# Attention and Mamba on one core: the Mamba layer's timetable drawn anew, with another first pair and another choice of products for GpSimd

## The chip, the core and the metric

The kernel runs on one core of a Trainium2 chip. A core has five engines with instruction queues of their own: TensorE (PE in the profile, its weight loads PEld), VectorE (DVE), ScalarE (ACT), GpSimd (POOL) and SyncE (SP), which here only issues DMAs. Each engine takes its instructions strictly in order, and an instruction starts when the semaphores that it waits for have been reached. The metric is the time of one execution on the device in microseconds; lower is better.

## The reference

A batch of 128 images of 128 channels and 32 x 32 pixels goes through two layers, all in fp32. The first is an attention over the batch at each pixel, with a residual and a layer norm. The second is a Mamba block on each image's 1024 pixels, taken as a sequence:

```python
xh = einsum('oi,bihw->bohw', cv1_w, x) + cv1_b
l  = silu(batchnorm(depthwise_conv3x3(xh)))
t  = layernorm(xh as tokens)
xm, z = split(t @ in_proj_w.T)                     # 256 channels each
xm = silu(causal_conv1d(xm, 4 taps) + conv1d_b)
dt, Bm, Cm = split(xm @ x_proj_w.T)                # 8, 16, 16
dt = softplus(dt @ dt_proj_w.T + dt_proj_b)
h[s] = exp(dt * A) * h[s-1] + dt * Bm * xm         # 256 channels x 16 states
y  = (h * Cm).sum(states) + xm * D
g  = (y * silu(z)) @ out_proj_w.T
out = x + cv2_w @ concat(l, g) + cv2_b
```

The costly part is the recurrence: 256 x 16 sequences of 1024 steps in each of 128 images.

## The kernel before

The attention layer runs first and leaves its result in DRAM (`mid`). It takes about the first 2900 us, and nothing in it is touched here. The Mamba layer then works on the images one after another, overlapped in time.

Of an image the recurrence makes 32 **units** of 128 x 1024: half `h` of the channels (two), group `nb` of four states (four), and block `db` of 32 channels (four). Two blocks form a pair, A (blocks 0 and 1) or B (2 and 3), and `PAIRS` (L367) lists the 16 pairs of an image in their order, such as `A1`: block pair A, states 1. Unit `k` belongs to pair `k // 2`. A unit consists of these tasks (`unit`, L1197, inside `units`, L1190):

- **decay k** on ScalarE (L1241): exp(dt x A) from `dtr`, the copy of dt that a load has spread to 128 partitions.
- its **inputs** dt x B x xm: for 20 units GpSimd makes two at once (`b_poolk`, L1216, `dtxr` times `brep` into one of three `dbu` buffers); for the 12 units of the pairs in `TENSOR` (L372) TensorE makes them by eight transposes of a prepared tile `bx` (`b_tensork`, L1209). TensorE writes into one of two PSUM tiles `da`, which alternate by unit. The decay takes the other place, `da` or `dbu`.
- **scan k** on VectorE (L1254): the recurrence itself.
- **product k**, h times C (L1262): on GpSimd for the units in `ON_POOL` (then the scan has written SBUF), on VectorE for the others (then the scan has written `da`).
- **sums** (L1281): for each half and state group, TensorE adds four units' products into `y_ps`. The products wait in eight `hc` buffers, taken in turn, so scan `k` may need the sums of unit `k - 8`.

Around the units stand, for the image itself, the `gate` (L1321), the sigmoid of z (`z_mm`, L909, into two PSUM banks, and `silu_z`, L926), `silu_l` and the outputs (`o_first`, `o_second`, `o_copy`); and for the next images the layer norm (`norm_mm`, `squared`, `variance`, `rstd`, `normed`), the causal convolution (`xm_mm`, `xm_copy`), the 3x3 convolution (`taps`, `l_copy`), and dt, B and C: `d_mm` (L954), `d_copy` (L970), `a_mm` (L983), four `softplus` (L998), `b_mm` and `b_copy` (L1045), then `dt_store`, `dtx_mul` on GpSimd (L1025) and `dtx_store`. ScalarE loads an activation table before the sigmoids, one after `silu_l`, one before softplus and one after it (1.28 us each).

dt, dt x xm, B and C are stored to DRAM and loaded again, spread over partitions, by SyncE's queue: `load_dt` and `load_dtx` (L1071, 1 MB each; two halves `j`, one for the A pairs and one for B, for each `h`), `load_b` and `load_c` (L1104, L1111, half a megabyte each).

The order on every engine is written out by hand or by a planner outside the file: the dictionary `AT` gives each task a moment in its image's timetable, and image `i` begins at `i * PERIOD`.

```python
t.at = t.image * PERIOD + AT[t.name]                       # L337
...
for t in sorted(self.tasks, key=lambda t: (t.at, t.place)):  # L356
```

The numbers only sort. The program is emitted in that order, so each engine's queue is that order, and when a task runs is left to the semaphores on the chip.

Of the kernel before, what the change touches and what calls it, by code (L numbers as in the profile page):

```python
# [324 lines left out]
class Plan:  # L325
# [43 lines left out]
    for h, some in enumerate(['A1 A2 B2 B1 A3 A0 B3 B0', 'A0 A1 B0 B1 A2 A3 B2 B3'])  # L369
# [7 lines left out]
ON_POOL = [0, 1, 2, 3, 5, 8, 10, 11, 12, 13, 14, 15, 18, 19, 23, 25, 26, 27]  # L377

PERIOD = 96.19
AT = {  # L380
    "a_mm00": -44.86, "a_mm01": -43.94, "a_mm10": -40.89, "a_mm11": -40.09, "b_copy": -37.27,
    "b_mm": -38.14, "b_pool0": -11.59, "b_pool6": 2.5, "b_pool8": 14.73, "b_pool12": 21.64,
    "b_pool18": 45.47, "b_pool22": 50.01, "b_pool24": 56.93, "b_pool26": 68.6, "b_pool28": 73.15,
    "b_pool30": 77.69, "b_tensor2": 2.41, "b_tensor3": 0.28, "b_tensor4": 6.97, "b_tensor5": 4.86,
    "b_tensor10": 29.61, "b_tensor11": 27.54, "b_tensor14": 38.87, "b_tensor15": 35.79,
    "b_tensor16": 43.3, "b_tensor17": 40.35, "b_tensor20": 56.91, "b_tensor21": 53.12,
    "bc_store": -31.86, "d_copy": -45.59, "d_mm": -47.72, "decay0": -2.15, "decay1": -5.96,
    "decay2": -0.53, "decay3": -11.29, "decay4": 7.68, "decay5": 3.95, "decay6": 17.31,
    "decay7": 12.43, "decay8": 24.71, "decay9": 18.35, "decay10": 28.35, "decay11": 27.31,
    "decay12": 34.25, "decay13": 31.47, "decay14": 29.39, "decay15": 30.43, "decay16": 38.19,  # L390
    "decay17": 37.15, "decay18": 51.1, "decay19": 48.51, "decay20": 47.47, "decay21": 52.14,
    "decay22": 63.5, "decay23": 61.02, "decay24": 69.99, "decay25": 67.67, "decay26": 75.38,
    "decay27": 72.31, "decay28": 81.79, "decay29": 77.7, "decay30": 89.02, "decay31": 83.25,
    "dt_store0": -40.28, "dt_store1": -10.23, "dtx_mul0": -34.72, "dtx_mul1": -2.29,
    "dtx_store0": -32.21, "dtx_store1": 9.24, "gate0": 49.49, "gate1": 108.33, "l_copy0": -3.86,
    "l_copy1": -4.92, "load_b0": -27.4, "load_b1": 22.22, "load_b2": -1.78, "load_c0": -3.58,
    "load_c1": -12.03, "load_c2": -7.18, "load_c3": 7.44, "load_dt00": -19.55, "load_dt01": -5.38,
    "load_dt10": 29.62, "load_dt11": 36.91, "load_dtx00": -22.92, "load_dtx01": -13.83,
    "load_dtx10": 19.4, "load_dtx11": 38.71, "norm_mm0": -132.98, "norm_mm1": -98.77,
    "normed0": -125.31, "normed1": -89.36, "o_copy0": 131.83, "o_copy1": 117.14,  # L400
    "o_first0": 126.95, "o_first1": 111.81, "o_second0": 129.82, "o_second1": 114.47,
    "out_store0": 132.7, "out_store1": 118.02, "pad_mm0": -92.28, "pad_mm1": -90.19,
    "padded0": -91.2, "padded1": -89.11, "product0": 19.27, "product1": 0.13, "product2": 12.35,
    "product3": 7.05, "product4": 13.35, "product5": 9.98, "product6": 20.99, "product7": 16.98,
    "product8": 28.5, "product9": 24.88, "product10": 33.6, "product11": 31.23,
    "product12": 38.35, "product13": 35.98, "product14": 43.09, "product15": 40.72,
    "product16": 48.27, "product17": 47.06, "product18": 63.86, "product19": 54.56,
    "product20": 61.3, "product21": 57.68, "product22": 67.81, "product23": 66.23,
    "product24": 73.72, "product25": 82.24, "product26": 91.53, "product27": 89.16,
# [1079 lines left out]
```

## Time and profile before

| | |
|---|---|
| time, median of 3 runs | 15043.29 us |
| lowest, highest | 15040.22, 15054.52 us |
| profiled execution: time, span | 15073.08 us, 15071.3 us |
| VectorE busy | 13733.7 us, 91% |
| TensorE busy | 13455.7 us, 89% |
| GpSimd busy | 12317.6 us, 82% |
| ScalarE busy | 12058.3 us, 80% |

The page shows one execution; the median is of other executions. Shares are over the whole span, attention included: in its first fifth GpSimd is hardly used, in the rest it is busy 9 tenths and more in every slice. A row of groups gives line, engine, operation, written and read tiles, shapes and count, then busy time in us and the mean of one in ns, then the idle time of the engine just before such instructions with what ended it. A row of the timeline gives start, duration, engine, line and tiles, and in brackets an idle time before it. In the view of windows the columns are the window, its length, the busy time of PE, PEld, DVE, ACT and POOL with their instructions, the granted TensorE clock, the DMA share and GB/s.

### The profile page before, as it was taken

To read this page: it belongs to the slowest core of one execution; us is meant where nothing else is said; L and a number is where in the kernel's file an instruction comes from. 1 tells how busy PE (TensorE), PEld (TensorE's weight loads), DVE (VectorE), ACT (ScalarE), POOL (GpSimd) and SP (SyncE) were. 2 spreads that over 40 slices of the span, in tenths; PEclk is the share of its full clock that TensorE was granted. 3 is DMA by queue.
4 is the path that set the end of the run, shared out by engine and by line. 5 is a ranking of instruction groups with operands and counts; after the bars stand their busy time and mean duration, and the time that the engine had idled before them with its cause. 6 is when DMAs were issued, how large, how long until landed. Compare 5 with 4: busy or idle time off the path is not lost. (4 is left out here: it accounts for less than half of the span.)

```text
span 15071.3 us, 229111 instructions
## 1 busy us (share of the span) xinstructions
PE 13455.7 (89%) x87094; PEld 6624.5 (44%) x87094; DVE 13733.7 (91%) x8754; ACT 12058.3 (80%) x19718; POOL 12317.6 (82%) x4361
## 2 busy tenths in 40 slices
PE   9999999888888888888888888888888888888887
PEld 6666666433333333333333333333333333333333
DVE  6777777599999999999999999999999999999999
ACT  5666666688888888888888888888888888888887
POOL 1222222299999999999999999999999999999999
PEclk9999999899999999999999999999999999999999
DMA  3222222266676666666666666666666666666665
GB/s 57 50 57 46 46 46 46 67 169 169 169 169 169 168 169 169 168 168 169 169 168 168 168 168 169 168 169 168 169 167 169 168 168 169 169 169 169 167 168 146
DMA packets 1191603, 2180.96 MB, mean 145 GB/s; under 512 B 673233, under 2 KB 674273, under 8 KB 1190497
## 3 DMA queue, kind: packets, MB, share of 16 engines
q1 hardware_dynamic: 1190496, 2166.31, 59.6%
q8 instruction: 682, 11.17, 0.3%
q14 instruction: 425, 3.47, 0.1%
HBM read 1746.30 MB, written 419.43 MB: 144 GB/s over the span
## 5 line engine op out<-in xcount | busy, mean ns | idle before, releaser
L1216 POOL TENSOR_TENSOR dbu<-dtxr,brep 128x2048 f32<-128x2048 f32 x1280 | 5805.4, 4552 | 27.7 <-DMA dtr<-dtd 13.3
L1262 POOL TENSOR_TENSOR hc<-hc,crep 128x1024 f32<-128x1024 f32 x2304 | 5412.3, 2372 | 310.5 <-PE da L1209 211.1
L1241 ACT ACTIVATE da<-dtr,aneg 128x1024 f32<-128x1024 f32 x2560 | 2956.6, 1163 | 510.3 <-DVE hc L1262 489.3
L1254 DVE TENSOR_TENSOR_SCAN hc<-da,dbu 128x1024 f32<-128x1024 f32 x1408 | 3162.1, 2276 | 103.6 <-ACT da L1241 94.9
L1155 ACT ACTIVATE bx<-p_ps,bT 128x128 f32<-128x128 f32 (+1 forms) x8192 | 2798.0, 486 | 132.1 <-PE p_ps L1147 131.9
L1254 DVE TENSOR_TENSOR_SCAN da<-da,dbu 128x1024 f32<-128x1024 f32 x1152 | 2622.7, 2287 | 115.3 <-ACT da L1241 106.9
L1209 PE MATMUL da<-ident,bx 128*128 128x128 f32 x12288 | 1828.7, 295 | 501.1 <-DVE hc L1254 417.6
L1209 PEld LDWEIGHTS da<-ident,bx 128*128 128x128 f32 x12288 | 1489.7, 150 | 1634.3 <-DVE hc L1254 1068.5
L1262 DVE TENSOR_TENSOR hc<-da,crep 128x1024 f32<-128x1024 f32 x1792 | 2162.8, 1219 | 47.8 <-PE y_ps L1281 6.5
L769 PE MATMUL p_ps<-tn,wk 128*128 128x512 f32 x4096 | 1989.5, 608 | 240.4 <-DVE tn L733 147.2
L1241 ACT ACTIVATE dbu<-dtr,aneg 128x1024 f32<-128x1024 f32 x1536 | 1734.3, 1218 | 473.2 <-DMA dtr<-dtd 471.1
L1254 DVE TENSOR_TENSOR_SCAN hc<-dbu,da 128x1024 f32<-128x1024 f32 x896 | 2000.1, 2268 | 24.3 <-ACT dbu L1241 21.4
L1281 PE MATMUL y_ps<-hc,fold 128*32 128x512 f32 x16384 | 1974.3, 599 | 37.6 <-POOL hc L1262 25.8
L1254 DVE TENSOR_TENSOR_SCAN da<-dbu,da 128x1024 f32<-128x1024 f32 x640 | 1451.1, 2282 | 196.4 <-PE da L1209 132.6
L221 POOL COPY xg<-xt 128x512 f32<-128x512 f32 x256 | 270.4, 1057 | 1223.2 <-PE m_ps L217 1199.3
L830 PE MATMUL p_ps<-xpad,dwd 64*64 64x512 f32 x9216 | 1153.4, 593 | 112.8 <-ACT xm L801 105.3
L769 PEld LDWEIGHTS p_ps<-tn,wk 128*128 128x128 f32 x4096 | 710.6, 191 | 1141.6 <-issue 776.3
L243 POOL TENSOR_SCALAR yt<-z,nw,nb 128x512 f32<-128x512 f32 x256 | 320.2, 1251 | 1032.7 <-DVE z L242 1032.7
L1281 PEld LDWEIGHTS y_ps<-hc,fold 128*32 128x32 f32 x16384 | 477.0, 109 | 1182.9 <-issue 858.3
L830 PEld LDWEIGHTS p_ps<-xpad,dwd 64*64 64x64 f32 x9216 | 362.4, 133 | 802.4 <-issue 568.4
L1025 POOL TENSOR_TENSOR dtt<-dtt,xm 128x1024 f32<-128x1024 f32 x256 | 608.5, 2377 | 120.9 <-DMA dtd<-dtt 109.8
L203 DVE TENSOR_TENSOR oT<-m_ps,rden 128x512 f32<-128x512 f32 x256 | 177.0, 691 | 566.2 <-ACT rden L202 566.2
(131 smaller groups left out, 19281.3 us busy)
## 6 DMA issues: line engine op xcount, KB each, us to landing
dtxr<-dtxd SPq DMA_DIRECT2D x2048, 256.0 KB, 5.5
dtr<-dtd SPq DMA_DIRECT2D x2048, 256.0 KB, 5.4
crep<-bcd SPq DMA_DIRECT2D x2048, 128.0 KB, 6.2
brep<-bcd SPq DMA_DIRECT2D x1536, 128.0 KB, 5.0
x<-mid SPq DMA_DIRECT2D x256, 512.0 KB, 5.9
dtd<-dtt SPq DMA_DIRECT2D x256, 512.0 KB, 5.2
dtxd<-dtt SPq DMA_DIRECT2D x256, 512.0 KB, 4.4
xt<-in_x SPq DMA_DIRECT2D x64, 1024.0 KB, 12.2
```

Of the source, the lines that this page charges most:

```text
L221: nc.gpsimd.tensor_copy(xgs[p % 4].rearrange("c (l b) -> c l b", l=LG), pixels(xts, p))
L243: nc.gpsimd.tensor_scalar(pixels(yts, y), z.rearrange("c (l b) -> c l b", l=LG), nw, nb, ALU.mult, ALU.add,)
L769: nc.tensor.matmul(a.tile, lhsT=wk[:, k, h * P : (h + 1) * P], rhs=tn[:, c * CH + k : (c + 1) * CH + k], start=k == 0, stop=c > 0 and k == ...
L830: nc.tensor.matmul(pair[r] .tile[c * HP : (c + 1) * HP] .rearrange("p (r q) -> p r q", q=HH), lhsT=dwd[rs, k, :], rhs=xpad[rs, y0 : y0 + r ...
L1025: lambda: nc.gpsimd.tensor_mul(dtt[h], dtt[h], im["xm"][h]),
L1155: nc.scalar.activation(bx[:, tb, ks, n, :], src, AF.Copy, scale=bT[:, j : j + 1])
L1209: nc.tensor.transpose(ps[:, tb * P : (tb + 1) * P], bx[:, tb, TENSOR[h, nb] * NDB + db].rearrange("p n d -> p (n d)"), ident,)
L1216: nc.gpsimd.tensor_mul(dbu[u // 2 % NDBU], dtxr[db // 2], brep[nb - 1].unsqueeze(1).to_broadcast([P, 2, L]),)
L1241: lambda: nc.scalar.activation(a, dtr[db // 2][:, db % 2, :], AF.Exp, scale=aneg[:, h * NDB + db, nb : nb + 1],),
L1254: lambda: nc.vector.tensor_tensor_scan(dst, a, b, 0.0, ALU.mult, ALU.add),
L1262: lambda: engine.tensor_mul(hc[u % 8], dst, crep[nb]),
L1281: nc.tensor.matmul(y_ps[db * GD : (db + 1) * GD, chunk(c)], lhsT=fold, rhs=hc[(i * NG + k) % 8][:, chunk(c)], start=False, stop=last,)
```

## The change

The two constants and the whole timetable are replaced; no function changes. In the first half of an image `A2` now comes before `A1`. So units 0 and 1 are units whose inputs TensorE makes (`b_tensor0`, `b_tensor1`), and units 2 and 3 have a pair of GpSimd's (`b_pool2`). `ON_POOL` has 19 units instead of 18: 4, 16, 21, 24 and 30 come in, 5, 15, 23 and 26 go out. `AT` has the same tasks but for those names, at other moments, and so another order on each engine. The core of the diff, with the lines that the prediction speaks of:

```diff
@@ -366,7 +366,7 @@
-    for h, some in enumerate(['A1 A2 B2 B1 A3 A0 B3 B0', 'A0 A1 B0 B1 A2 A3 B2 B3'])
+    for h, some in enumerate(['A2 A1 B2 B1 A3 A0 B3 B0', 'A0 A1 B0 B1 A2 A3 B2 B3'])
@@ -374,64 +374,64 @@
-ON_POOL = [0, 1, 2, 3, 5, 8, 10, 11, 12, 13, 14, 15, 18, 19, 23, 25, 26, 27]
+ON_POOL = [0, 1, 2, 3, 4, 8, 10, 11, 12, 13, 14, 16, 18, 19, 21, 24, 25, 27, 30]
-PERIOD = 96.19
+PERIOD = 94.66
...
-    "b_tensor16": 43.3, "b_tensor17": 40.35, "b_tensor20": 56.91, "b_tensor21": 53.12,
+    "b_tensor15": 41.17, "b_tensor16": 42.34, "b_tensor17": 47.31, "b_tensor20": 54.77,
+    "b_tensor21": 59.11, "bc_store": -43.47, "d_copy": -44.15, "d_mm": -46.19, "decay0": -2.38,
...
-    "sums10": 64.75, "sums11": 69.91, "sums12": 90.68, "sums13": 94.53, "taps0": -14.18,
+    "softplus11": -36.36, "squared0": -127.55, "squared1": -89.95, "sums00": 50.41,
+    "sums01": 27.39, "sums02": 22.78, "sums03": 43.48, "sums10": 67.78, "sums11": 75.14,
...
-    "xm_mm111": -86.2, "xm_mm112": -85.14, "xm_mm113": -84.09, "z_mm00": 36.94, "z_mm01": 37.97,
-    "z_mm10": 41.5, "z_mm11": 42.4,
+    "xm_mm113": -79.34, "z_mm00": 39.18, "z_mm01": 40.22, "z_mm10": 45.41, "z_mm11": 46.37,
```

The order that follows from it, around the places that the prediction works out (tasks of the next image marked with ', of the image after it with "):

| engine | before | after |
|---|---|---|
| TensorE | `b_tensor14`, `b_tensor17`, `z_mm10`, `z_mm11`, `b_tensor16`, `sums03`, `sums00`, `d_mm'`, `a_mm00'`, `a_mm01'`, `b_tensor21`, `a_mm10'`, `a_mm11'`, `b_tensor20`, `b_mm'`, `norm_mm0"` | `b_tensor15`, `b_tensor16`, `sums03`, `z_mm10`, `z_mm11`, `b_tensor17`, `d_mm'`, `sums00`, `a_mm00'`, `a_mm01'`, `b_tensor20`, `a_mm10'`, `a_mm11'`, `b_mm'`, `b_tensor21`, `norm_mm0"` |
| ScalarE | `silu_z10`, `silu_z11`, `silu_l`, decays 20 and 19, `d_copy'`, decays 18 and 21, softplus' (four), `b_copy'`, `squared0"`, decay 23, `rstd0"`, decay 22 | `silu_z10`, `silu_z11`, `silu_l`, `d_copy'`, decays 18, 19 and 20, softplus' (four), `b_copy'`, decay 21, `squared0"`, decay 22, `rstd0"`, decay 23 |
| GpSimd | products 13, 12, 15, 14, pairs 18, 22, product 19, pair 24, `dtx_mul0'`, products 18, 23, pairs 26, 28, 30, product 25, pair 0', products 27, 26 | products 13, 14, pair 18, product 16, pairs 22, 24, `dtx_mul0'`, products 21, 18, 19, pairs 26, 28, 30, products 25, 24, 27, 30, pair 2' |
| SyncE | `load_dtx01'`, `load_c1'`, `dt_store1'`, `load_c2'`, `load_dt01'` | `load_dtx01'`, `load_b2'`, `dt_store1'`, `load_c1'`, `load_dt01'` |

On VectorE each image's scans now run in the order of their numbers; before, the odd one of a pair mostly came first.

## The prediction

> **What bounds the kernel now.** I read the page first (engine totals, slices), then the groups between 4000 and 14000 us with shapes kept apart, then the busy time within one image, and last one image instruction by instruction. From slice 9 on the page repeats itself: 128 images in one rhythm. The same scan starts in image 119 99 x 94.63 us after it starts in image 20, so an image costs **94.63 us**, and all below is per image.
>
> The groups (busy us, mean ns | idle time before them, and who ended it), and the busy time within one image:
>
> ```profile
> L1216 POOL TENSOR_TENSOR dbu<-dtxr,brep 128x2048 f32<-128x2048 f32 x1057 | 4794.2, 4552 | 11.2 <-DVE da L1254 10.3 <-DMA dtxr<-dtxd 0.3 <-POOL hc L1262 0.2
> L1262 POOL TENSOR_TENSOR hc<-hc,crep 128x1024 f32<-128x1024 f32 x1904 | 4472.7, 2372 | 256.0 <-PE da L1209 173.3 <-DVE hc L1254 76.8 <-DMA brep<-bcd 0.4
> ...
> L1262 DVE TENSOR_TENSOR hc<-da,crep 128x1024 f32<-128x1024 f32 x1480 | 1786.3, 1219 | 36.3 <-PE y_ps L1281 2.2
> ```
> ```profile
> core 0: us, PE busy (x) PEld busy (x) DVE busy (x) ACT busy (x) POOL busy (x), PEclk, DMA share, GB/s
> 9007.13:9101.76 94.63, 82.31 (x420) 36.92 (x420) 90.84 (x50) 79.17 (x133) 91.85 (x31) 0.96 0.70 169
> ```
>
> VectorE (90.8) and GpSimd (91.9) both fill the image to 4%. Neither is the bound alone: each loses about 3 us to short waits on the other, on ScalarE, on TensorE and on the loads of `dtr`. A change that moves work between the two is decided by the waits it leaves.
>
> **The change, part by part.**
>
> *Products.* Five move to GpSimd (4, 16, 21, 24, 30), four come back to VectorE (5, 15, 23, 26). Back to back, GpSimd takes 2.33 us for a product (seven in 16.35; less the last one's 2.37, over six) and 4.49 for an input pair (three in 13.50). Its floor becomes 10 x 4.49 + 21 x 2.33 (19 products, two `dtx_mul`) = **93.8 us**; it was 91.5. VectorE loses 1.14 us, start to start, and needs 89.8. So GpSimd has the least room, and the gain can't pass 0.83 us.
>
> *A rule against it.* The row: the product takes 2.37 us on GpSimd and 1.22 on VectorE. The Trainium skill (GPSIMD Engine Reference, section 4.1, Engine selection) puts elementwise work on VectorE because of such a ratio. Obeyed, no product moves, and the sum stays at 94.63.
>
> *The pair order.* Units 0 and 1 now take their inputs from TensorE, units 2 and 3 from GpSimd; there are still 12 such units and ten pairs. The pair that opened the image was ready 5 us before its scan, so its going saves nothing by itself.
>
> *The timetable.* No task is added on TensorE, ScalarE or the load queue; their order is new. I followed it along GpSimd's queue with the trace's starts and durations, and asked of each product and pair when its inputs come if GpSimd never pauses. Most come early: product 8 by 4 us, 10 to 14 by 1.4 to 1.9, pairs 26, 28 and 30 by 3 or more, `dtx_mul0` and `dtx_mul1` by about 2. Those moves cost nothing while that lead lasts, and each us beyond it counts once per image. Two places have no lead.
>
> *Place 1, product 13 to product 21.* TensorE's new order is `b_tensor16`, `sums03`, `z_mm10`, `z_mm11`, `b_tensor17`, `d_mm`. `sums03` waits for product 13, and the second half of the gate's matmuls, ahead of it until now, is queued behind. Behind these on ScalarE stand the gate's sigmoids, `silu_l`, `d_copy`, decays 18 to 20, the softplus, `b_copy` and decay 21; scan 21 waits for that, and product 21, new on GpSimd, for the scan. The prices (start, duration):
>
> ```profile
> 9050.99 1.25 ACT L874 ACTIVATE l<-l,bnt,bns 128x1024 f32<-128x1024 f32 x1
> 9052.26 1.28 ACT L877 ACT_TABLE_LOAD   x1
> ...
> 9055.70 0.59 ACT L970 COPY xp<-p_ps 128x512 f32<-128x512 f32 x1
> 9056.18 1.13 ACT L1241 ACTIVATE da<-dtr,aneg 128x1024 f32<-128x1024 f32 x1
> 9057.24 1.14 ACT L1241 ACTIVATE dbu<-dtr,aneg 128x1024 f32<-128x1024 f32 x1
> 9058.39 1.28 ACT L998 ACT_TABLE_LOAD   x1
> 9059.68 1.27 ACT L998 ACTIVATE dtt<-p_ps,dtb 128x512 f32<-128x512 f32 x2
> 9062.35 1.45 ACT L998 ACTIVATE dtt<-p_ps,dtb 128x512 f32<-128x512 f32 x2 [1.40 <-PE p_ps L983]
> 9063.82 1.28 ACT L877 ACT_TABLE_LOAD   x1
> 9065.86 0.27 ACT L1045 COPY bT<-p_ps 128x32 f32<-128x32 f32 x2 [0.76 <-PE p_ps L1040]
> ```
>
> From product 13's end: 0.05 to the start of `sums03`, 1.74 for it, 1.96 to the end of `z_mm11` (all start to start on TensorE), 0.08 to the sigmoid, 0.57, 1.27 for `silu_l`, 1.30 for the table: `d_copy` at 6.97. Then 0.48, 1.05 + 1.05 (decays 18, 19), 2.44 (decay 20 and a table): softplus at 11.99. To its fourth part 2.67 + 0.76, then 1.99 (0.71 and a table; the 0.76 wait for `b_mm` goes, as `b_tensor21` no longer stands ahead of it), 0.2 for `b_copy`, 1.18 for decay 21, 2.27 for scan 21, 0.13 to GpSimd: **21.18**. GpSimd would be there after 3 x 4.49 + 3 x 2.33 = 20.46 (pairs 18, 22, 24, products 14, 16, `dtx_mul0`), less 0.02. It waits **0.74**.
>
> In that sum 2.67 + 0.76 is a price at half clock:
>
> ```profile
> 9056.34 1.13 PE L983 MATMUL p_ps<-xp,dtwT 8*128 8x512 f32 x4 [0.69 <-ACT xp L970]
> 9058.63 1.09 PE L1209 MATMUL da<-ident,bx 128*128 128x128 f32 x8 [1.16 <-DVE hc L1254]
> 9060.43 2.65 PE L983 MATMUL p_ps<-xp,dtwT 8*128 8x512 f32 x4 [0.70 <-ACT dtt L998]
> ```
> ```profile
> 9056.00:9060.00 4.00, 2.22 (x12) 1.16 (x12) 4.00 (x3) 3.97 (x5) 4.00 (x2) 1.00 0.01 2
> 9060.00:9063.00 3.00, 2.57 (x4) 0.81 (x4) 2.97 (x3) 1.60 (x3) 3.00 (x3) 0.61 0.40 165
> 9063.00:9067.00 4.00, 4.00 (x15) 2.95 (x14) 3.19 (x2) 2.29 (x5) 4.00 (x2) 0.50 0.02 7
> ```
>
> After two short idles (1.16 and 0.70 us) the granted clock, last number but two, falls to 0.50, and the same four matmuls take 2.65 instead of 1.13 us. In the new order TensorE idles more there, about 1.7 and 0.7 us, so I take half clock. The Trainium skill (TensorE: Matmul & The Clock Gate, Why this matters for your kernels) asks only that idle gaps stay under about 3 us. By that rule the clock would hold, softplus would be 1 us shorter, no wait would be left, and the sum would be 93.8 us an image; the row contradicts it, and I go by the row. In before the half clock sets in between 1.9 us ahead of the softplus and 1.3 behind; about one image in seven should get it too late to matter: -0.10 on the mean.
>
> *Place 2, product 21 to product 30.* GpSimd needs 6 x 2.33 + 3 x 4.49 = 27.45, to 48.63 on the same scale. On the other side, at half clock: softplus 10 done at 15.4, `b_mm` 0.86, `b_tensor21` 1.76, 1.95 to `squared0` (20.0), 1.91 in this image and 2.19 on the mean to `rstd0`, 2.39 to scan 23 (24.3 to 24.6). From there VectorE is full for 21.9 us to scan 30, plus 2.40: 48.6 to 48.9. I take **0.10** of these 0 to 0.3.
>
> *Start and end.* The first image begins with other inputs, and the last product runs on GpSimd beside VectorE's last. Either is an edge of one image, between -8 and +5 us by the idle times around the first scan; I take 0.
>
> **Sum.** 93.8 + 0.74 + 0.10 - 0.10 = 94.54 us, against 94.63: -0.09 x 127 = -11 us. The profiled execution took 15073.1 us (span 15071.3), 30 more than the median; -11 leads it to 15062 and the median of 15043 to **15032 us**. A measurement here can tell about 0.2% (30 us) from no change, so that is "the same".
>
> **The rivals.** *TensorE keeps its clock, or ScalarE catches up* (faster): GpSimd runs without a pause, 93.8 to 94.3 us, 14938 to 15005 us. For it: softplus at full clock removes all of place 1. Against: every image of the trace has such a half-clock stretch, and the new order idles there more.
>
> *The load of `dtr` for decay 4 comes too late* (slower). Decay 4 is now the first reader of the second half, the buffer is freed by decay 31, the image's last, and `load_c1` stands ahead in the queue. In before the same 3.5 MB of loads took 19.2 us from the first issue, and ScalarE idled 1.6 us for them. In after they land 6.2 (by the freeing) to 9.0 us (by the backlog) after scan 0 starts. From 9.1 us on it decides: VectorE's 0.8 us of room up to scan 8 is gone by then, and each us counts in full. At 9.7 it is +0.6: 95.1 us, 15105.
>
> *It only exchanges waits* is my forecast: 94.3 to 94.85 us, 15005 to 15070.
>
> **How the numbers follow.** Forecast 0.40, faster rival 0.32, slower one with other late loads 0.28; the three signs have the same chances. The range takes in most of both rivals: 14948 to 15110.
>
> **What would show it.** Right: GpSimd busy about 94 of 94.5 us, VectorE about 90; an idle of some 0.7 us before product 21, ended by scan 21, and softplus with 2.7 us from first to third part at half clock. Wrong: full clock there and no idle on GpSimd (faster), or ScalarE idle for `dtr` before decay 4 and TensorE or VectorE late at scan 8 (slower).

## The result and the profile after

| | before | after |
|---|---|---|
| median of the runs taken together | 15047.81 us (15040.22 to 15054.52) | 15233.96 us (15230.87 to 15238.07) |
| ratio | | **1.0126**, 95% interval 1.0113 to 1.0138 |
| profiled execution, span | 15073.08, 15071.3 us | 15234.04, 15232.3 us |
| one image (scan 0 to scan 0, images 20 to 119) | 94.63 us | 95.97 us |
| GpSimd waits per image before product 21, before product 30 | (other order) | 1.87, 0.29 us |

The changed kernel is 1.26% slower. In the two profiled executions, 161 us apart, an image takes 1.34 us more, 170 us over 127 images. Positions and waits of single tasks, here and below, are means over images 20 to 119, worked out from each trace.

First the groups of GpSimd, one of ScalarE and one of VectorE between 4000 and 14000 us (busy us, mean ns | idle before, and who ended it), and the busy time of all engines over the same 10 ms (columns as in the prediction):

```profile
L1216 POOL TENSOR_TENSOR dbu<-dtxr,brep 128x2048 f32<-128x2048 f32 x1043 | 4724.2, 4550 | 0.1
L1262 POOL TENSOR_TENSOR hc<-hc,crep 128x1024 f32<-128x1024 f32 x1981 | 4630.2, 2376 | 224.0 <-DVE hc L1254 221.0 <-DMA dtxr<-dtxd 2.3
```
```profile
L1241 ACT ACTIVATE dbu<-dtr,aneg 128x1024 f32<-128x1024 f32 x1251 | 1414.0, 1165 | 271.4 <-DMA dtr<-dtd 254.8 <-issue 8.7 <-ACT x L1369 3.3
```
```profile
L1254 DVE TENSOR_TENSOR_SCAN hc<-dbu,da 128x1024 f32<-128x1024 f32 x833 | 1877.4, 2274 | 311.5 <-ACT dbu L1241 296.3 <-PE da L1209 13.5
```
```profile
4000.00:14000.00 10000.00, 8789.68 (x43766) 3890.36 (x43765) 9373.87 (x5109) 8265.68 (x13770) 9773.92 (x3232) 0.95 0.69 166
```

GpSimd is now the bound: 9774 of 10000 us busy, and its input pairs wait for nothing (0.1 us). All that it loses stands before products, 224 us in 104 images (2.15 us each), and is ended by scans. So 93.8 us of work and 2.17 us of waits make the image. The reader should see the chain behind it in the other two groups: scans wait for decays written into `dbu`, and those decays wait for loads of `dtr`.

One image (62, in which the wait is somewhat longer than the mean) shows it in order: ScalarE, then GpSimd and VectorE (start, duration).

```profile
8936.88 0.59 ACT L970 COPY xp<-p_ps 128x512 f32<-128x512 f32 x1
8937.36 2.16 ACT L1241 ACTIVATE da<-dtr,aneg 128x1024 f32<-128x1024 f32 x2
8941.09 1.15 ACT L1241 ACTIVATE dbu<-dtr,aneg 128x1024 f32<-128x1024 f32 x1 [1.57 <-DMA dtr<-dtd]
8942.26 1.28 ACT L998 ACT_TABLE_LOAD   x1
8943.56 1.26 ACT L998 ACTIVATE dtt<-p_ps,dtb 128x512 f32<-128x512 f32 x2
8946.40 1.27 ACT L998 ACTIVATE dtt<-p_ps,dtb 128x512 f32<-128x512 f32 x2 [1.58 <-PE p_ps L983]
8947.69 1.28 ACT L877 ACT_TABLE_LOAD   x1
8948.98 0.27 ACT L1045 COPY bT<-p_ps 128x32 f32<-128x32 f32 x2
8949.14 1.16 ACT L1241 ACTIVATE dbu<-dtr,aneg 128x1024 f32<-128x1024 f32 x1
```
```profile
8947.94 2.34 POOL L1025 TENSOR_TENSOR dtt<-dtt,xm 128x1024 f32<-128x1024 f32 x1
8952.70 4.65 POOL L1262 TENSOR_TENSOR hc<-hc,crep 128x1024 f32<-128x1024 f32 x2 [2.42 <-DVE hc L1254]
```
```profile
8950.33 2.29 DVE L1254 TENSOR_TENSOR_SCAN hc<-dbu,da 128x1024 f32<-128x1024 f32 x1 [2.71 <-ACT dbu L1241]
8953.50 2.30 DVE L1254 TENSOR_TENSOR_SCAN da<-da,dbu 128x1024 f32<-128x1024 f32 x1 [0.88 <-ACT da L1241]
```

Decay 20 (8941.09) stands 1.57 us for its load (mean 1.04), the softplus, decay 21 and scan 21 follow later by as much, and GpSimd, free since 8950.28, waits for product 21 until 8952.70. The load in question, `load_dt11`, is the last of four of 1 MB that stand close together: `load_dt10` waits for its buffer until decay 11 ends (30.8 us after scan 0), `load_dtx10` stands behind it, though its buffer is free, then `load_dtx11` and `load_dt11`. They land at 37.9, 42.5, 48.5 and 53.1 us. In before `load_dtx10` was issued ahead (18.9 us) and `load_dt11` had landed at 42.4.

The softplus shows the other cost, TensorE's half clock (TensorE's instructions, then stretches of the same image; the granted clock is the last number but two):

```profile
8940.92 1.09 PE L1209 MATMUL da<-ident,bx 128*128 128x128 f32 x8 [1.55 <-DVE hc L1254]
8944.30 2.65 PE L983 MATMUL p_ps<-xp,dtwT 8*128 8x512 f32 x4 [2.28 <-ACT dtt L998]
```
```profile
8941.00:8945.00 4.00, 1.72 (x10) 1.41 (x11) 4.00 (x3) 3.70 (x4) 4.00 (x2) 0.68 0.08 31
8945.00:8953.00 8.00, 7.02 (x19) 3.82 (x18) 4.88 (x3) 5.16 (x8) 5.58 (x3) 0.50 0.32 131
```

### The profile page after: what moved, and what is told of

Same layout as the page of the kernel before. It is cut to its first block, busy times and chain, and to the rows that moved or that the text cites. A ratio compares the mean times of both kernels' runs of the same rounds, so it can differ in the third digit from the quotient of the medians.

```text
span 15232.3 us, 228981 instructions
## 1 busy us (share of the span) xinstructions
PE 13597.8 (89%) x87094; PEld 6612.9 (43%) x87094; DVE 13597.9 (89%) x8626; ACT 12062.5 (79%) x19718; POOL 12594.9 (83%) x4489
## 5 line engine op out<-in xcount | busy, mean ns | idle before, releaser
L1262 POOL TENSOR_TENSOR hc<-hc,crep 128x1024 f32<-128x1024 f32 x2432 | 5684.4, 2376 | 278.0 <-DVE hc L1254 272.4
L1216 POOL TENSOR_TENSOR dbu<-dtxr,brep 128x2048 f32<-128x2048 f32 x1280 | 5797.5, 4550 | 16.7 <-DMA dtr<-dtd 13.5
L1241 ACT ACTIVATE da<-dtr,aneg 128x1024 f32<-128x1024 f32 x2560 | 2911.5, 1141 | 1105.1 <-DVE hc L1262 657.0
L1155 ACT ACTIVATE bx<-p_ps,bT 128x128 f32<-128x128 f32 (+1 forms) x8192 | 2758.0, 462 | 15.0 <-PE p_ps L1147 13.3
L1254 DVE TENSOR_TENSOR_SCAN hc<-dbu,da 128x1024 f32<-128x1024 f32 x1024 | 2307.9, 2274 | 407.4 <-ACT dbu L1241 387.7
L769 PE MATMUL p_ps<-tn,wk 128*128 128x512 f32 x4096 | 1929.2, 603 | 287.7 <-ACT xpad L754 143.1
L1281 PE MATMUL y_ps<-hc,fold 128*32 128x512 f32 x16384 | 2122.4, 600 | 24.3 <-POOL hc L1262 24.3
L1262 DVE TENSOR_TENSOR hc<-da,crep 128x1024 f32<-128x1024 f32 x1664 | 2017.6, 1219 | 74.9 <-DVE da L1254 24.8
L1254 DVE TENSOR_TENSOR_SCAN da<-dbu,da 128x1024 f32<-128x1024 f32 x512 | 1167.4, 2280 | 108.7 <-PE da L1209 108.7
```

Source lines behind the costliest of these rows:

```text
L769: nc.tensor.matmul(a.tile, lhsT=wk[:, k, h * P : (h + 1) * P], rhs=tn[:, c * CH + k : (c + 1) * CH + k], start=k == 0, stop=c > 0 and k == ...
L1155: nc.scalar.activation(bx[:, tb, ks, n, :], src, AF.Copy, scale=bT[:, j : j + 1])
L1216: nc.gpsimd.tensor_mul(dbu[u // 2 % NDBU], dtxr[db // 2], brep[nb - 1].unsqueeze(1).to_broadcast([P, 2, L]),)
L1241: lambda: nc.scalar.activation(a, dtr[db // 2][:, db % 2, :], AF.Exp, scale=aneg[:, h * NDB + db, nb : nb + 1],),
L1254: lambda: nc.vector.tensor_tensor_scan(dst, a, b, 0.0, ALU.mult, ALU.add),
L1262: lambda: engine.tensor_mul(hc[u % 8], dst, crep[nb]),
```

## The experiments

Numbers are those of the order in which they ran. Each run is compared with runs of the kernel before on the same chip. "Clock" is the time per image that TensorE had half clock. Waits are GpSimd's, in us per image; a dash is under 0.1, "n" not taken.

| | edit (on the changed kernel unless said) | median us | ratio to before, 95% | image | product 21 | product 30 | clock |
|---|---|---|---|---|---|---|---|
| - | changed kernel | 15234.0 | 1.0126 (1.0113 to 1.0138) | 95.97 | 1.87 | 0.29 | 10.6 |
| 1 | `load_dtx10` first | 15185.5 | 1.0089 (1.0072 to 1.0106) | 95.58 | 0.88 | 0.82 | 14.2 |
| 2 | gate matmuls first | 15273.4 | 1.0148 (1.0132 to 1.0163) | 96.29 | 1.88 | 0.28 | n |
| 3 | 1 and 2 | 15395.5 | 1.0227 (1.0212 to 1.0242) | 97.28 | 1.32 | 0.51 | 13.0 |
| 4 | before, with the new choice | 16057.8 | 1.0668 (1.0652 to 1.0684) | 102.40 | n | n | n |
| 5 | the old choice | 16046.3 | 1.0658 (1.0640 to 1.0676) | 102.37 | n | n | n |
| 6 | 1, 8-row filler | 15466.6 | 1.0274 (1.0259 to 1.0290) | 97.88 | 3.36 | 0.48 | 13.5 |
| 7 | 1, decays 21 to 23 ahead | 15402.4 | 1.0230 (1.0215 to 1.0245) | 97.35 | 2.82 | 0.42 | 13.3 |
| 8 | 6 and 7 | 15585.7 | 1.0351 (1.0336 to 1.0367) | 98.66 | 4.02 | 0.43 | 15.5 |
| 9 | 1, four whole-row fillers | 15276.2 | 1.0144 (1.0127 to 1.0161) | 96.22 | 2.05 | - | 3.9 |
| 10 | 9, two more fills | 15289.4 | 1.0151 (1.0136 to 1.0166) | 96.35 | 2.08 | 0.13 | 1.8 |
| 11 | 1, decays 22, 23 ahead | 15148.3 | 1.0058 (1.0043 to 1.0073) | 95.31 | 0.93 | 0.41 | 12.7 |
| 12 | 1, two whole-row fillers | 15063.6 | 0.9998 (0.9988 to 1.0007) | 94.51 | 0.36 | - | 3.4 |
| 13 | 12 and 11 | 15061.1 | 0.9996 (0.9986 to 1.0005) | 94.57 | 0.37 | 0.27 | 5.5 |
| 14 | 13, `load_c1` behind `load_dt01` | 15054.5 | 0.9994 (0.9985 to 1.0003) | 94.59 | 0.44 | 0.32 | 5.6 |
| 15 | 1, one filler, `load_c1` as in 14 | 15011.6 | 0.9970 (0.9959 to 0.9982) | 94.19 | 0.23 | 0.24 | 5.8 |
| 16 | 15, filler of one and a half | **14965.0** | **0.9941 (0.9927 to 0.9954)** | 93.88 | - | - | 2.9 |
| 17 | before, two whole-row fillers | 15154.1 | 1.0064 (1.0051 to 1.0077) | 95.35 | n | n | 3.5 |
| 18 | 16 without the edit of 1 | 15006.3 | 0.9969 (0.9959 to 0.9980) | 94.03 | 0.23 | - | 2.8 |

At the outset there were three theories. **The late load**: decay 20's wait for `dtr`. **The matmuls**: the forecast's own place 1, the gate's matmuls queued behind `sums03`. **The choice**: 19 products are too many for GpSimd in any order.

**1. `load_dtx10` ahead of `load_dt10`.**

```diff
-    "load_dtx01": -9.97, "load_dtx10": 33.7, "load_dtx11": 39.48, "norm_mm0": -128.63,
+    "load_dtx01": -9.97, "load_dtx10": 25.0, "load_dtx11": 39.48, "norm_mm0": -128.63,
```

> The changed kernel with one load moved in SyncE's queue: dtx of quarter 10 is issued ahead of dtr of quarter 10 instead of behind it. Late load (my theory): the load of dtr for decay 20 is the last of four 1 MB loads that stand close together and lands when the decay has already waited 1.04 us; one load fewer in front of it takes that wait away, and everything behind it up to product 21 comes 1 us earlier, so GpSimd's wait before product 21 falls from 1.87 to about 0.8 us, the period from 95.97 to about 94.9 us, the time by 1.04 x 127 = 132 us to about 15,100 us. Matmuls alone (the load is only where the chain happens to pause): GpSimd's wait stays within 0.2 us of 1.87 and the time within 25 us of 15,234 us. Choice too full (19 products on GpSimd simply do not fit, wherever the orders stand): the time falls by less than 25 us too.

Decay 20 no longer waits, and product 21's wait falls from 1.87 to 0.88, as the first theory had it. But the image falls by 0.39 us only, not by 1.04: the wait before product 30 grew from 0.29 to 0.82. GpSimd's product group, between 4000 and 14000 us, still idles 1.7 us an image:

```profile
L1262 POOL TENSOR_TENSOR hc<-hc,crep 128x1024 f32<-128x1024 f32 x1989 | 4645.5, 2371 | 178.7 <-DVE hc L1254 161.8 <-DMA dtxr<-dtxd 15.7 <-DMA brep<-bcd 1.2
```

In one image of it ScalarE still waits at the softplus and at the next image's norm, both for TensorE:

```profile
9113.76 1.14 ACT L1241 ACTIVATE dbu<-dtr,aneg 128x1024 f32<-128x1024 f32 x1
9114.92 1.28 ACT L998 ACT_TABLE_LOAD   x1
9116.21 1.26 ACT L998 ACTIVATE dtt<-p_ps,dtb 128x512 f32<-128x512 f32 x2
9119.23 1.26 ACT L998 ACTIVATE dtt<-p_ps,dtb 128x512 f32<-128x512 f32 x2 [1.76 <-PE p_ps L983]
...
9124.54 0.69 ACT L716 ACTIVATE tn<-p_ps,b1c 128x512 f32<-128x512 f32 x1 [1.41 <-PE p_ps L706]
```

**2 and 3. The gate's matmuls ahead of `sums03`; both moves.**

```diff
-    "xm_mm113": -79.34, "z_mm00": 39.18, "z_mm01": 40.22, "z_mm10": 45.41, "z_mm11": 46.37,
+    "xm_mm113": -79.34, "z_mm00": 39.18, "z_mm01": 40.22, "z_mm10": 43.42, "z_mm11": 43.45,
```

> The changed kernel with the two gate matmuls of the second pair moved on TensorE ahead of the sums that wait for product 13, and nothing else. Late load: decay 20 still cannot start before its dtr lands, so the chain from there to product 21 stands where it stood and the time stays within 20 us of 15,234 us. Matmuls alone: the sigmoids and what follows no longer wait for product 13, about 1.07 us of the chain go (the sums' 0.5 and the two matmuls), GpSimd's wait before product 21 falls to about 0.8 us and the time by about 136 us to about 15,098 us. Choice too full: less than 25 us either way.

> Both moves together: dtx of quarter 10 loaded ahead of dtr of quarter 10, and the gate matmuls ahead of the sums. Late load with the matmuls next behind it: both delays go, GpSimd's wait before product 21 falls from 1.87 us to 0 to 0.2, the period to 94.0 to 94.3 us (GpSimd's own 93.8 and the small wait before product 30), the time to 14,985 to 15,025 us, below the kernel before. Matmuls alone: as the second kernel, about 15,098 us. Choice too full: above 15,190 us.

Both got slower, and no theory had that. The gate's matmuls need a PSUM bank that ScalarE's first sigmoids free. Put ahead, they stand for the bank, the sums queue behind them, and scan 16 needs those sums (TensorE, then VectorE, in the second kernel):

```profile
9136.13 1.99 PE L909 MATMUL p_ps<-tn,inzT 128*128 128x512 f32 x4 [0.18 <-ACT sz L926]
9138.04 1.92 PE L1281 MATMUL y_ps<-hc,fold 128*32 128x512 f32 x16
```
```profile
9140.08 2.29 DVE L1254 TENSOR_TENSOR_SCAN hc<-dbu,da 128x1024 f32<-128x1024 f32 x1 [1.84 <-PE y_ps L1281]
```

Scan 16 waits 1.79 us on the mean in the second kernel and 3.24 in the third, where decay 17 also waits 1.33 us for `load_dt10` (1.22 in the first kernel, whose move makes that load land later, and 0.27 in after). The order "sums first" was not a fault: the place where the forecast saw the delay can't be had cheaper by this swap.

**4 and 5. Choice and timetable crossed.** Four: before with the new `ON_POOL`, shown here; five: the changed kernel with the old one, the same lines the other way round, and products 4 (to 14.0) and 24 (to 73.8) moved up.

```diff
-ON_POOL = [0, 1, 2, 3, 5, 8, 10, 11, 12, 13, 14, 15, 18, 19, 23, 25, 26, 27]
+ON_POOL = [0, 1, 2, 3, 4, 8, 10, 11, 12, 13, 14, 16, 18, 19, 21, 24, 25, 27, 30]
...
-    "product12": 38.35, "product13": 35.98, "product14": 43.09, "product15": 40.72,
+    "product12": 38.35, "product13": 35.98, "product14": 43.09, "product15": 40.3,
...
-    "product24": 73.72, "product25": 82.24, "product26": 91.53, "product27": 89.16,
+    "product24": 73.72, "product25": 82.24, "product26": 79.0, "product27": 89.16,
```

> The kernel before, its timetable and its pair order, with only the changed kernel's choice of GpSimd's products (19 in place of 18; products 15 and 26, now VectorE's, move up to where the scans leave them). Late load: the choice is not what costs; the loads stand as before and GpSimd's own work of 93.8 us a period sets the pace with small waits, 94.0 to 94.6 us a period, 14,970 to 15,045 us. Choice too full: slower than before by about what the changed kernel is, 15,190 to 15,240 us. If VectorE and GpSimd wait for each other at new places in an order drawn for other products, anything up to 15,250 us could come, and then the waits of the profile must say which.

> The changed kernel, timetable and pair order, with the kernel before's choice of GpSimd's products (18: products 5, 15, 23, 26 for GpSimd and 4, 16, 21, 24, 30 for VectorE; products 4 and 24, now VectorE's, move up to where the scans leave them). Choice too full: GpSimd's own work is 91.5 us a period, product 21 is no longer one that it waits for, VectorE's holes before scans 21 to 23 are made up later, and the period falls below before's 94.63 us, 14,900 to 15,040 us. Late load and what stands behind it: the chain to scan 21 is as late as it was and VectorE, with one product more, has nothing to make it up with; 95 to 96 us a period, 15,110 to 15,240 us. As the fourth kernel went (choice alone on before's timetable: 102.4 us), an order drawn for other products can also cost several us at places that neither theory names; then the run tells only that choice and timetable cannot be parted.

Both take 102.4 us an image; in the fourth GpSimd idles 8.6 us of them, mostly for scans. Here neither timetable carries the other's choice, so these two say nothing on the choice. That 19 products do fit was shown later, by the sixteenth.

**6 and 9. A filler for TensorE.** In the first kernel TensorE stands 1.55 us for scan 18 (as in the stretch of after above), and the clock falls there. Both kernels fill that time without changing the result: the sixth issues the small matmul `a_mm01` five times, the ninth issues four matmuls on whole rows into the same bank, which `a_mm01` then overwrites.

The sixth, in the task `a_mm` of `delta` (the operands of the matmul stay as they are), and the ninth at the same place:

```diff
+WARM = 5
...
-                    lambda c=c: nc.tensor.matmul(
+                    lambda c=c: [
+                        nc.tensor.matmul(
...
+                        for _ in range(WARM if (h, c) == (0, 1) else 1)
+                    ],
```
```diff
+FILL = 4
...
-                    lambda c=c: nc.tensor.matmul(
+                    lambda c=c: [
+                        nc.tensor.matmul(
+                            pair[c].tile, lhsT=ident, rhs=im["xm"][0][:, chunk(c)],
+                            start=True, stop=True,
+                        )
+                        for _ in range(FILL if (h, c) == (0, 1) else 0)
+                    ]
+                    + [
+                        nc.tensor.matmul(
...
+                    ],
```

> The first kernel (dtx of quarter 10 loaded ahead of dtr) with TensorE kept busy in the 1.5 us in which it waits for scan 18: the small matmul ahead of that wait is issued five times over, with the same result. Clock theory: after the load, what delays product 21 and then scans 22 and 23 is TensorE's half clock, which in the first kernel begins in that idle time and lasts about 10 us in each image; kept at full clock the softplus parts lie 1.8 us apart and not 2.8, decay 21 starts 1.2 us earlier, the norm's matmuls 1 to 2 us earlier, product 21's wait goes from 0.88 to about 0 and product 30's from 0.82 to at most 0.2, the period from 95.58 to 93.8 to 94.2 us, the time to 14,960 to 15,010 us. Order theory (what is late is the place of the decays in ScalarE's order, not the clock): the repeated matmul changes nothing by more than 0.3 us a period, 15,150 to 15,225 us.

> The first kernel with TensorE's wait for scan 18 filled as in the sixth, but by four matmuls that use all 128 rows of the array (into the same bank, overwritten by the real matmul behind them), where the sixth repeated one of 8 rows. In the sixth the clock fell to half at the same place although TensorE had run without a gap. Rows count: each matmul's time weighted by the share of the array that it uses, the clock fell in the runs so far only after a 3.41 us stretch below about 0.47 and rose only after one above 0.78; filled with whole rows the half clock no longer begins at 53 us after scan 0, the softplus parts lie about 1.8 us apart instead of 2.8, product 21's wait goes from 0.88 to below 0.3; the period falls from 95.58 to 94 to 95 us (how much depends on whether the half clock then begins a few us later, under the norm of the next image), 14,980 to 15,110 us. Rows do not count (the repeated matmuls were merely in the way): the clock falls at 53 us all the same, softplus 00's second part waits as in the sixth, 15,400 to 15,500 us.

The sixth (TensorE's instructions and a stretch of one image): the clock falls although TensorE runs without a gap.

```profile
9262.50 6.44 PE L985 MATMUL p_ps<-xp,dtwT 8*128 8x512 f32 x12
9268.88 1.97 PE L1213 MATMUL da<-ident,bx 128*128 128x128 f32 x8
```
```profile
9265.00:9269.00 4.00, 4.00 (x6) 1.12 (x5) 3.42 (x3) 1.86 (x3) 4.00 (x2) 0.51 0.10 40
```

The ninth, the same place with whole rows:

```profile
9146.49 3.70 PE L985 MATMUL p_ps<-xm,ident 128*128 128x512 f32 x8
```
```profile
9148.00:9151.00 3.00, 3.00 (x8) 0.93 (x6) 3.00 (x3) 1.77 (x2) 3.00 (x2) 1.00 0.11 45
```

Full clock, and half clock per image down from 14.2 to 3.9 us. So rows count. Yet the ninth is slower than the first: four such matmuls are eight records that start 0.43 us apart, 3.7 us in a gap of 1.55, and the second softplus part waits 1.3 us for them. The filler's size was my error; in the sixth it was the same.

**7, 8 and 11. Decays ahead on ScalarE.**

Seven; eight is seven with the sixth's filler; eleven leaves decay 21 where it was:

```diff
-    "decay21": 60.48, "decay22": 62.36, "decay23": 64.86, "decay24": 69.75, "decay25": 71.97,
+    "decay21": 57.0, "decay22": 60.6, "decay23": 62.5, "decay24": 69.75, "decay25": 71.97,
```
```diff
-    "decay21": 60.48, "decay22": 62.36, "decay23": 64.86, "decay24": 69.75, "decay25": 71.97,
+    "decay21": 60.48, "decay22": 61.5, "decay23": 62.9, "decay24": 69.75, "decay25": 71.97,
```

> The first kernel with three decays moved on ScalarE alone: decay 21 ahead of the third softplus part, decay 22 ahead of the squared values of the next image's norm, decay 23 ahead of its rstd. Order theory: scans 22 and 23 no longer wait 0.85 and 0.81 us, product 30's wait goes from 0.82 to about 0, product 21's from 0.88 to 0.5 (TensorE's transposes for scan 21 end only 0.35 us before decay 21 did), the period from 95.58 to about 94.4 us, the time to 15,020 to 15,060 us. Clock theory: the same 0.5 stays at product 21, as the transposes at half clock now bind alone; if the half clock lies under scans 22 and 23 too, less than half of product 30's wait goes and the time stays above 15,110 us.

> The first kernel with both: the repeated matmul and the three decays moved. If clock and order are two parts of one sum, GpSimd is left with its own work, 93.8 to 94.0 us a period, 14,955 to 14,985 us, about 0.5% below the kernel before. If the sixth kernel alone reaches that, the decays' places were only a consequence of the clock, and this one is within 15 us of it.

> The first kernel with decays 22 and 23 alone moved ahead on ScalarE (ahead of the squared values and of the rstd of the next image's norm); decay 21 stays, since between two softplus parts it cost two loads of ScalarE's function tables in the seventh kernel. Order theory: scans 22 and 23 no longer wait (0.85 and 0.81 us), product 30's wait goes from 0.82 to below 0.2, product 21's stays at 0.88, the period falls from 95.58 to about 94.9 us, the time by 70 to 100 us to about 15,100 us. Clock theory: less than half of that.

Seven and eight came out some 350 and 600 us above the gains expected of them, and the trace shows a reason that lies in the edit: an exponential between two softplus parts costs two table loads (ScalarE in the seventh).

```profile
9226.23 1.28 ACT L1241 ACT_TABLE_LOAD   x1
9227.52 1.15 ACT L1241 ACTIVATE dbu<-dtr,aneg 128x1024 f32<-128x1024 f32 x1
9228.69 1.28 ACT L998 ACT_TABLE_LOAD   x1
```

The eleventh, without that, gains 0.27 us an image on the first by the traces (some 50 us by the medians, each against its own runs of before), between the two theories: product 30's wait halves, product 21's stays. So order seems not to be the larger part.

**10. Two further fills** on the ninth: transposes for scan 21 ahead of `b_mm`, and `norm_mm0` issued three times.

```diff
-    "b_tensor21": 59.11, "bc_store": -43.47, "d_copy": -44.15, "d_mm": -46.19, "decay0": -2.38,
+    "b_tensor21": 57.8, "bc_store": -43.47, "d_copy": -44.15, "d_mm": -46.19, "decay0": -2.38,
...
-                lambda: nc.tensor.matmul(
-                    a.tile, lhsT=w1cT, rhs=x[:, chunk(c)], start=True, stop=True
-                ),
+                lambda: [
+                    nc.tensor.matmul(
+                        a.tile, lhsT=w1cT, rhs=x[:, chunk(c)], start=True, stop=True
+                    )
+                    for _ in range(1 if c else 3)
+                ],
```

> The ninth kernel, and the two idle stretches of TensorE that follow filled too: the transposes for scan 21 ahead of those of B and C, and the norm's first matmul issued three times. If the half clock only moved in the ninth to the norm, it goes here: product 30's wait below 0.3 us, the period 93.8 to 94.3 us, 14,955 to 15,020 us. If the ninth already has no half clock under the path, this one is within 30 us of it; if the transposes for scan 21 now stand in the way of those of B and C, ScalarE waits for B and C before decay 21 and product 21's wait is back at 0.5 or more, 15,060 to 15,150 us.

Half clock falls to 1.8 us an image, and the time stays 13 us above the ninth's: removing what was left gained nothing, net of what the extra fills cost. The two were not parted.

**12, 13, 14. The filler at its right length, and what adds to it.**

Twelve is the ninth with two matmuls; thirteen adds the eleventh's decays; fourteen adds the load:

```diff
-FILL = 4
+FILL = 2
```
```diff
-    "load_c0": -28.15, "load_c1": -6.02, "load_c2": -0.62, "load_c3": 1.18, "load_dt00": -15.14,
+    "load_c0": -28.15, "load_c1": -4.0, "load_c2": -0.62, "load_c3": 1.18, "load_dt00": -15.14,
```

> The ninth kernel with two whole-row matmuls in TensorE's wait for scan 18 in place of four. The ninth showed the half clock gone from the softplus parts, but each of the four took two records of 0.43 us, 3.4 us in all for an idle stretch of 1.55, so that softplus 00's second part waited 1.3 us for them; two take 1.7 us. Clock theory: the third softplus part follows the first by 1.8 to 2.0 us in place of 2.8, product 21's wait falls from 0.88 to 0 to 0.4, and the period from 95.58 to 94.3 to 95.0 us (the half clock that begins a little later may keep part of product 30's 0.82), 15,020 to 15,110 us. If the clock cost nothing on the path: within 25 us of the first kernel's 15,186.

> The twelfth kernel with decays 22 and 23 ahead of the next norm's two activations, as in the eleventh. Clock and order as two parts of one sum: product 30's wait below 0.3 and product 21's as in the twelfth; 94.0 to 94.6 us a period, 14,980 to 15,060 us. If the eleventh's gain (0.27 us a period) was only what the clock had left, nothing is added to the twelfth.

> The thirteenth kernel with one load moved on SyncE's queue: that of C for state block 1 behind that of dtr for decay 4 (it is issued just ahead of it and waits for its buffer until 1 us before scan 0; in the kernels that got faster behind, decay 4 then waited up to 2 us and scan 4 up to 1.2). My second rival's mechanism: VectorE's wait before scan 4 goes (0.3 to 1.2 us), and with it what VectorE lacks further on; 93.9 to 94.2 us a period, 14,960 to 15,010 us, 0.3 to 0.6% under the kernel before. If scan 4's wait is made up before product 10 in any case, as it was in the changed kernel: within 15 us of the thirteenth.

The twelfth gains 1.07 us an image on the first: the clock is the larger cost. GpSimd's product group:

```profile
L1272 POOL TENSOR_TENSOR hc<-hc,crep 128x1024 f32<-128x1024 f32 x2012 | 4710.5, 2390 | 52.8 <-DVE hc L1264 49.1 <-DMA dtxr<-dtxd 1.2
```

178.7 us of idle are 52.8. The decays' order adds nothing once the clock is held (thirteenth), which speaks for the eleventh's gain being a part of the clock's cost. In the thirteenth decay 4 waits 1.7 us for its load (2.2 in the twelfth); the fourteenth has none of that wait and is 7 us under the thirteenth, less than the runs can tell: it seems to be made up before GpSimd feels it.

**15 and 16. A shorter filler** (on the first kernel with `load_c1` as in 14).

Fifteen, and what sixteen adds between the filler and the real matmul:

```diff
-FILL = 2
+FILL = 1
```
```diff
+                    + [
+                        nc.tensor.transpose(
+                            pair[c].tile[:, q * P : (q + 1) * P],
+                            im["xm"][0][:, q * P : (q + 1) * P], ident,
+                        )
+                        for q in range(4 if (h, c) == (0, 1) else 0)
+                    ]
```

> The twelfth kernel with the load of C for state block 1 behind that of dtr for decay 4 (as in the fourteenth) and one whole-row matmul as filler in place of two. In the fourteenth the filler still ended 0.65 us after TensorE's wait for scan 18 would have, so that the third softplus part came 1.25 us after ScalarE was free; product 21 then waited 0.44 us. Clock held: the third part comes 0.6 us earlier, product 21's wait goes from 0.4 to 0, the period to 94.0 to 94.2 us, 14,990 to 15,025 us, under both kernels. Clock not held (one matmul of 0.86 us is too little for the 3.41 us stretch, whose weighted use is about 0.45 then, at the edge): the half clock is back at 53 to 56 us after scan 0 in many images, product 21's wait stays at 0.4 or grows, 15,050 to 15,180 us.

> The fifteenth with four transposes of 0.11 us on whole rows beside the one matmul, a filler of 1.3 us. Between the fourteenth and the fifteenth: if the clock is held by 1.3 us and not by 0.86, this is the faster of the two, 14,995 to 15,040 us; if both hold it, 0 to 25 us slower than the fifteenth.

One matmul holds the clock in part (5.8 us of half clock an image); one and a half hold it better (2.9 us), and end early enough. The sixteenth beats both kernels, and came out 30 us under the expected range. Its groups on GpSimd, and the 10 ms:

```profile
L1233 POOL TENSOR_TENSOR dbu<-dtxr,brep 128x2048 f32<-128x2048 f32 x1067 | 4841.1, 4560 | 1.3 <-DVE hc L1271 1.2
L1279 POOL TENSOR_TENSOR hc<-hc,crep 128x1024 f32<-128x1024 f32 x2024 | 4731.9, 2384 | 9.6 <-DVE hc L1271 6.1
```
```profile
4000.00:14000.00 10000.00, 9036.31 (x45354) 3919.87 (x45353) 9563.92 (x5220) 8430.17 (x14065) 9989.13 (x3304) 0.98 0.70 170
```

9989 of 10000 us: next to nothing can be won now without taking work off GpSimd.

**17. The same filler in before** (two matmuls, nothing else).

> The kernel before, its own timetable, pair order and choice, with the filler of two whole-row matmuls in TensorE's wait (1.16 us there). In the kernel before the half clock lies under the softplus parts too (9.4 us of each period), and VectorE waits 1.03, 0.60 and 0.49 us before scans 20, 23 and 22 behind it. If the clock is worth there what it was worth between the first kernel and the twelfth (0.96 us a period), 14,940 to 14,990 us; if VectorE and GpSimd make the waits up further on (GpSimd waits 2.0 us before product 8 whatever comes), within 30 us of the kernel before.

A miss on both sides: 0.72 us an image slower. Half clock falls from 9.4 to 3.5 us, and the waits before scans 20, 23 and 22 (2.1 us) go. But before scan 21 a new one of 1.08 us for TensorE appears (the gap there is 1.16 us, the filler longer), and scan 4's grows from 0.48 to 1.71, as decays 5 and 4 wait longer for their load:

```profile
L1251 ACT ACTIVATE dbu<-dtr,aneg 128x1024 f32<-128x1024 f32 x1259 | 1422.6, 1226 | 551.5 <-DMA dtr<-dtd 550.0
```

In before the same group idled 381 us. And the third softplus part still follows the first by 2.85 us (2.79 in before): this filler takes there what the full clock gives. So the run does not tell what a held clock is worth in before; a shorter filler there was not tried.

**18. The load put back** into the sixteenth (`load_dtx10` at 33.7 again).

> The sixteenth kernel, in which GpSimd waits for nothing, with the first experiment's move undone: dtx of quarter 10 is again loaded behind dtr of quarter 10. The load alone: dtr for decay 20 lands 53.1 us after scan 0 as in the changed kernel, decay 20 starts there at 53.3 in place of 52.9, nothing between it and product 21 has slack (scan 21 ends as GpSimd comes free), so GpSimd waits 0.4 to 0.6 us before product 21; 94.3 to 94.5 us a period, 15,020 to 15,045 us. If the load cost its whole 1.04 us wherever the rest stands: 15,090 to 15,100 us. If it lands no later than the decay wants it once the rest is on time: within 15 us of the sixteenth, and the first experiment's gain came from something else that the move touches.

44 us by the medians, each against its own runs of before (0.34 us an image; the runs lie between 14987 and 15018), 0.15 us an image in the profiled execution, the fastest of the eight. Product 21's wait is 0.23, under the 0.4 to 0.6 expected. By the medians the late load costs about a third of its 1.04 us here. The clock granted over a whole run goes from 0.983 in the shortest of the eight to 0.977 in the longest, so a part even of that can be the clock's.

## Why the prediction was wrong

**The sum's terms, on its own scale from product 13's end.** "The sum" is the prediction's; the first kernel is the one with the load mended.

| | the sum | after | first kernel | sixteenth |
|---|---|---|---|---|
| `d_copy` starts | 6.97 | 7.04 | 7.17 | 7.07 |
| decay 20 starts | 9.55 | **10.72** | 9.74 | 9.64 |
| softplus starts | 11.99 | 13.19 | 12.20 | 12.09 |
| `b_copy` starts | 17.40 | 18.62 | 17.67 | 16.77 |
| product 21 starts | 21.18 | 22.33 | 21.39 | 20.49 |
| `squared0` starts | 20.0 | 21.17 | 20.36 | 18.38 |
| `rstd0` starts | 21.9 to 22.2 | 23.22 | **22.89** | 20.34 |
| scan 23 starts | 24.3 to 24.6 | 25.61 | 25.27 | 22.88 |

*GpSimd's floor, 93.8 us.* Right: the sixteenth runs at 93.88 with 0.09 of waits left.

*"Most come early".* Right: in after products 8 and 10 to 14, the pairs and both `dtx_mul` wait 0.02 us or less. The two places named are the two where GpSimd waits.

*Place 1.* This step failed, in one term: "1.05 + 1.05 (decays 18, 19), 2.44 (decay 20 and a table): softplus at 11.99". It let decay 20 follow decay 19 at once. In its place stands a wait of 1.04 us for `load_dt11`; every other link agrees within 0.1 us, and the wait before product 21 was 1.87 in place of 0.74. These 1.13 us are most of the 1.43 between the sum (94.54) and the measured image (95.97); place 2 makes 0.19 and the discount 0.10. I had followed the load queue only to decay 4 (the second rival) and written of the rest that its order was new. The mechanism of that rival was the right one, at another load. At decay 4 itself it went as the rival's condition had it: landed at 8.5 us, under the 9.1 from which it would decide, scan 4 late by 0.46 us, scan 8 on time.

*The half clock at place 1.* Right in size: softplus to `b_copy` took 5.43 us in after, 5.41 in the sum. The discount of 0.10 for images that escape it was wrong: in each of the 100 images that stretch took 5.33 us or more.

*Place 2.* "I take 0.10 of these 0 to 0.3" measured 0.29, but that was luck: with product 21 late, GpSimd came late to product 30 as well. With the load mended it is 0.82. The term that was too small is "1.91 in this image and 2.19 on the mean to `rstd0`": 2.53 in the first kernel, where the half clock lasts on into `variance0` (mean granted clock between `squared0` and `rstd0` 0.67, in after 0.92). The links ahead of it add up to 0.36 more, as `squared0` starts at 20.36 in place of 20.0. So the load and this place were both mis-sized, and the first hid part of the second: taking away 1.04 us gave 0.39.

*Sum of what was found*: 95.97 - 0.39 (load) - 1.07 (clock, with the filler of 12) - 0.63 (12 to 16) = 93.88. As `load_c1` brought at most 0.06 us an image in 14, most of the 0.63 should be the filler's length; `load_c1` alone was not put back into 16. The parts depend on the order of removal, as 18 shows for the load.

*The faster rival*, full clock and no pause, gave 93.8 to 94.3 (by the sum's own scale 94.3 us are 15001 us, where the rival has 15005). The place it named was right and the price too, but in after TensorE did not keep the clock by itself: it took a filler to get there. With it the image takes 94.03 us even with the load left late (18), and 93.88 with the load moved as well (16).

*The rules.* That a product is better left on VectorE (the Trainium skill, GPSIMD Engine Reference, section 4.1) would have meant 94.63 us; the sixteenth has five moved, four back, and 93.88. The ratio of 2.37 to 1.22 us is real, but in before both engines had work for less than the image (91.9 and 90.8 of 94.63 us), and what decided here were the waits. What remains open is how choice and timetable share in this, as 4 and 5 could not part them, and whether the old timetable with a filler of the right length would do as well: 17 had only the longer one.

## What to carry to other kernels

A forecast that follows one engine's queue has to follow the DMA queue just as far: one load whose buffer is not yet free holds back those behind it, and here the fourth in a row arrived 1 us too late. Where two waits lie in series on a full engine, removing the first shows the second, so size each as if the other were gone. And before filling an idle engine, measure the filler: on the first kernel the same idea cost 0.5% with four matmuls (3.7 us) and gained 0.9% with two.

## What the runs showed of the hardware that I had not expected

- **The clock changes on a fixed grid, and goes with how much of the array is in use.** In before, after and the first, sixth and sixteenth kernels all changes of the granted clock in the Mamba layer lie on a grid of 3.4133 us, within 1 ns. The Trainium skill (TensorE: Matmul & The Clock Gate, What's actually happening) gives the same free-running window, 3413 ns. I weighted each matmul's time by rows and columns used over 128 x 128, overlapping ones added up to at most 1 (worked out from the traces). In these kernels the clock went from full to half only after a window of at most 0.52, and back only after one of at least 0.78. These are no sharp thresholds: windows from 0.42 on also left it at full, and windows up to 0.80 left it at half. By time alone, 99 of the 100 falls between images 20 and 119 of the sixth kernel follow windows that are busy to 99% or more: matmuls of 8 rows don't hold the clock. By this weighting the gaps of 1.2 to 1.6 us matter because the matmuls beside them use 8 of 128 rows: a window with 1.55 us idle and the whole array in use for the rest would weigh 0.55 (an estimate).
- An fp32 matmul of 512 columns on the whole array is two records that start 0.43 us apart at full clock (the ninth kernel), and `a_mm00` and `a_mm01`, on different rows of the array, run side by side (1.13 us for both). A filler between them parts them: 1.12 us each.
- Four 1 MB loads in a row land 4.6 to 6.0 us apart in after; a DMA of them (256 KB) lands up to 11.0 us after issue (all such loads between 4000 and 14000 us).
